# Moving the preparation of exponential tables to earlier batches of a projection stretch

## The chip, the core and the metric

The kernel runs on one core of one Trainium2 chip. A core has a tensor engine (PE, matrix products and transposes, with its weight loads shown as PEld), a vector engine (DVE), a scalar engine (ACT, activations and copies), GpSimd (POOL) and a queue engine (SP) that only issues transfers. Sixteen DMA engines move data between the chip's memory and the core. Each engine takes its own instructions in order; they wait for one another through semaphores. The metric is device time in microseconds (us), lower being better. All arrays are float32.

## The reference

The input x has 64 rows in the batch, 128 channels and 2048 steps in time. Two residual layers follow each other:

```python
# layer 0: each batch row picks one of 16 weight matrices of 128 x 128
x = x + einsum('bct,bcd->bdt', x, weights[condition])
# layer 1: a long convolution along time, one kernel K per channel, cut off at a length per row
dt  = exp(log_dt);  dtA = (-exp(log_A_real) + 1j * A_imag) * dt
Ct  = Cc * (exp(dtA) - 1) / A
K   = 2 * einsum('hn,hnl->hl', Ct, exp(dtA[:, :, None] * arange(2048))).real
y   = causal convolution of x with K, plus x * D
x   = x + y * (arange(2048) < length)
```

`exp(dtA * step)` is a damped turning number for each of 128 channels and 64 modes. The kernel does not convolve over all 2048 steps at once. It cuts time into chunks of 128 steps, uses a Toeplitz matrix inside a chunk, and carries 64 complex states from chunk to chunk. For both it needs tables of those turning numbers for 0 to 128 steps.

## The kernel before

**The two stretches.** Time is cut in two segments of 1024 steps. First, layer 0 is computed for segment 0 of all 64 rows ("batches" in the code, counted from 0): `batch0(b)`. After that the main loop goes over groups of channels; it computes layer 1 for both segments, and layer 0 for segment 1 in between. Layer 0 works with channels on the partitions and layer 1 with batch rows on them, so the result goes out to a scratch array `scr` in the chip's memory and comes back as `x` tiles. The first such load needs every row of segment 0.

**A batch of the first stretch.** `batch0(b)` does the following in order. Every second batch, SP fetches a pair of rows 9 pairs ahead (`xb`, 1 MB, ten buffers). POOL copies the weights of batch b + 3 (`weigh`; four buffers). PE makes two products of 128 x 512 into a PSUM tile (two of them alternate). An engine that is passed in as `copy` brings the tile back into `xb`, and the ACT queue stores 512 KB to `scr`. The default for `copy` is ACT.

**The preparation of the tables.** Between the batches, in an order that is written out by hand, the engines prepare the tables. `_Parameters` computes rates, frequencies and phases on DVE during batches 0 to 11. `exps(g)` writes the damping part of table g with four ACT exponentials; there are 16 tables `e`. `partial_angles(k)` for k = 0 to 5 forms partial turns on DVE in six steps, five of them over 128 x 1600 elements, in the tile `parts`. Then each table takes ten steps of its own, the dictionary `STEPS`: a PE transpose of a slice of `parts` (`turn_parts`, tile `pa`), its copy by ACT (`keep_parts`, tile `a`), a PE product that adds the partial turns (`add_parts`, tile `pt`), four small DVE steps (`angles`), two sines on ACT (`sines`), two products on DVE (`products`), eight small PE products with output weights (`lags`, tile `pk`), a copy by ACT, one DVE addition, and two POOL stores of the convolution kernel to `kpad`. The key of `STEPS` is the lag in batches behind the table's first step. A new table starts every second batch, beginning with batch `FIRST`.

**What sets the order.** Nothing is reordered by a scheduler. Each engine runs its instructions as the Python code emits them, and `manual_schedule` adds the semaphores. ACT needs a table load of its own whenever it changes between exponentials and sines.

**Lines of the change.** Lines 596 to 612 emit the parameters and batches 0 to 11; `exps(b - 6)` in batches 6 to 9 writes tables 0 to 3. Lines 743 to 777 are the loop over batches 12 to 63. In batches 12 to 17, the copy is DVE's, one step of `partial_angles` follows, and two tables of exponentials are written. POOL issues sixteen tiny loads of the gains `dcol` in batches 12 to 19, two a batch. The first table starts with batch 18; the last one, started with batch 48, ends its lags with batch 55 and its stores with batch 60.

Of the kernel before, what the change touches and what calls it, by code (L numbers as in the profile page):

```python
# [371 lines left out]
def cond_resid_ssm_kernel(  # L372
# [13 lines left out]
    nc = tc.nc  # L386
# [47 lines left out]
    def fetch(s, n):  # L434

        xbs[s, n] = big.tile([P, BT, SL], F32, tag="x", name=f"xb_{s}_{n}")
        src = x[n * BT : (n + 1) * BT, :, s * SL : (s + 1) * SL]
        nc.sync.dma_start(xbs[s, n], src.rearrange("b c t -> c b t"))

    def weigh(s, b, plus=None):  # L440

        w1s[s, b] = s0.tile([P, C], F32, tag="w1", name=f"w1_{s}_{b}")
        at = nc.values_load(
            ci[:, b : b + 1],
            engines=(mybir.EngineType.Pool,),
            min_val=0,
            max_val=S - 1,
            skip_runtime_bounds_check_because="it is clamped above",
        )
        w = wres[:, bass.ds(at, 1), :].rearrange("p s d -> p (s d)")  # L450
        if plus is None:
            nc.gpsimd.tensor_copy(w1s[s, b], w)  # L452
        else:
            nc.gpsimd.tensor_tensor(w1s[s, b], w, plus, ALU.add)

    def project(s, b, q, ps, n_banks=1, copy=nc.scalar.copy):

        n, r = divmod(b, BT)
        own = xbs[s, n][:, r, :]
        for k in range(n_banks):  # L460
            cols = slice((q + k) * BK, (q + k + 1) * BK)
            nc.tensor.matmul(ps[:, k], w1s[s, b], own[:, cols], start=True, stop=True)  # L462
        cols = slice(q * BK, (q + n_banks) * BK)
        copy(own[:, cols], ps.rearrange("p k t -> p (k t)"))  # L464
        if q + n_banks == QB:
            to = scr[s].rearrange("(f b) c t -> b c f t", f=2)[b]
            nc.scalar.dma_start(to, own.rearrange("c (f t) -> c f t", f=2))
            del w1s[s, b]
            if r == BT - 1:
                del xbs[s, n]  # L470

    def batch0(b, copy=nc.scalar.copy):
        if b % BT == 0 and b // BT + AHEAD < B // BT:
            fetch(0, b // BT + AHEAD)
        if b + WAHEAD < B:
            weigh(0, b + WAHEAD)
        project(0, b, 0, psp.tile([P, QB, BK], F32, tag="y", name=f"p0_0_{b}", bufs=2), QB, copy)

    V = nc.vector
    es = [tab.tile([P, TP, 2, NE], F32, tag=f"e{g}", name=f"e_{g}") for g in range(NT)]  # L480

    def par_of(row, g, i):
        return gtab[:, row, g * TP + i : g * TP + i + 1]

    def exps(g):

        for i in range(TP):
            nc.scalar.activation(es[g][:, i, 0, :], steps, AF.Exp, scale=par_of(DRE, g, i))
# [12 lines left out]
    with tc.tile_pool(name="setup", bufs=1) as setup:  # L501
# [47 lines left out]
        def run(chain, n=None):  # L549
            for _ in chain if n is None else zip(range(n), chain):  # L550
                pass
# [53 lines left out]
        par.lay("ppar_2", rows, 1, par.row(gtab, PHI))  # L605
        run(par.sizes())
        batch0(10)
        rows = par.spread("rows3", (par.amp, 1.0), (par.amp, -1.0), (par.lr, 1.0), (par.li, 1.0))
        batch0(11)
        par.lay("ppar_3", rows, 4, par.row(ptab, AMP), swapped=1)  # L610
        rows = par.spread("rows4", (par.wr, 1.0), (par.wi, 1.0))
        par.lay("ppar_4", rows, 2, par.weight)
# [9 lines left out]
    def partial_angles(k):  # L622

        own = parts[:, :, 0:NL]
        by_l = some_l.unsqueeze(1).to_broadcast([P, NP, NL])

        def of(row, n):
            return gtab[:, row, :].unsqueeze(2).to_broadcast([P, NP, n])

        if k == 0:  # L630
            V.tensor_tensor(own, of(FHI, NL), by_l, ALU.mult)
        elif k == 1:
            V.tensor_scalar(whole, own, MAGIC, MAGIC, ALU.add, ALU.subtract)
        elif k == 2:
            V.tensor_tensor(own, own, whole, ALU.subtract)
        elif k == 3:
            V.tensor_tensor(whole, of(FLO, NL), by_l, ALU.mult)
        elif k == 4:
            V.tensor_tensor(own, own, whole, ALU.add)
        else:  # L640
            V.tensor_tensor(parts[:, :, 0:8], parts[:, :, 0:8], of(PHI, 8), ALU.add)
            V.tensor_tensor(parts[:, :, 24:25], parts[:, :, 24:25], of(PHI, 1), ALU.add)
            V.tensor_scalar(last, parts[:, :, 24:25], MAGIC, MAGIC, ALU.add, ALU.subtract)
            V.tensor_tensor(last, parts[:, :, 24:25], last, ALU.subtract)
# [83 lines left out]
    def fetches(n):  # L728

        nonlocal begun  # L730
        while begun < min(n + BT * QB, len(pieces)):
            fetch(pieces[begun][0], pieces[begun][1] // BT)
            begun += BT * QB
# [7 lines left out]


    ps = {}
    FIRST = 18
    STEPS = {
        12: store_lags,
        10: gain_lags,
# [7 lines left out]
        0: turn_parts,  # L755
    }
    for now in range(12, B):
        batch0(now, V.tensor_copy if now < 18 else nc.scalar.copy)
        if now < 20:

            by_row = d_in.rearrange("(h j c d) -> c d j h", j=8, c=2, d=2)
            with nc.allow_non_contiguous_dma(reason="128 gains, four times"):
                for i, r in ((i, r) for i in range(TP) for r in range(4) if (i * 4 + r) // 2 == now - 12):
                    nc.gpsimd.dma_start(dcol[i * NR + r : (i + 1) * NR : 4, :], by_row[r % 2, r // 2])
        if now == 21:
            V.tensor_scalar(dcol, dcol, 1.0, None, ALU.add)
        if now < FIRST:
            partial_angles(now - 12)
        if now < 18:
            exps(2 * now - 20)  # L770
            exps(2 * now - 19)
        for lag, step in STEPS.items():
            g, odd = divmod(now - FIRST - lag, 2)
            if not odd and 0 <= g < NT:
                step(g)
        if now == 60:
            fetches(FILL)
# [232 lines left out]
```

## Time and profile before

| what | value |
|---|---|
| three runs, median (lowest to highest) | 1125.23 us (1122.19 to 1125.81) |
| the profiled execution, its own time | 1122.48 us |
| its span in the profile | 1120.7 us |
| PE busy, share of the span | 1076.6 us, 96% |
| DVE, ACT, POOL busy | 803.0, 680.7, 242.5 us |
| matmuls of layer 0 (`p`, L462) | 257.9 us, 512 records, 617 ns mean |
| exponentials of the tables (`e`, L488) | 64, 385 to 406 ns each, from 33.7 to 71.7 us |
| copies of `parts` slices (`a`, L653) | 16, 266 ns each, from 75.1 to 153.4 us |
| first load of `x` back from `scr` | issued at 186.19 us, landed 5.79 us later |

The span starts with the first instruction and ends with the last; the execution's own time is a little more. A line of the profile names the engine, the source line, the operation, and its output and input tiles. The chain of waits goes back from the last instruction to whatever released each step. A window row gives each engine's busy time in a stretch, the granted PE clock and what DMA moved. A record of a product of 512 columns is half of it: "p L462 x4" is one batch, that is two products.

### The profile page before, as it was taken

What the parts mean: (1) busy time and instruction counts of PE and PEld (TensorE: products, weight loads), DVE (VectorE), ACT (ScalarE), POOL (GpSimd) and SP (SyncE); (2) the same over time, 40 slices, a digit from 0 to 9 for tenths busy, and PEclk for the clock granted to TensorE, in tenths of its full rate; (3) what the DMA queues carried; (4) which work ended last, traced back from release to release, by engine and by line L of the source; (5) the groups of instructions that cost most, each with busy time, mean ns of one, the idle gap of its engine ahead of it and who ended that gap; (6) DMA issues with size and microseconds to landing.
All of it is one profiled execution on the core that took longest, in us unless ns stands there. A gap on an engine that the chain in (4) does not pass through costs nothing.

```text
span 1120.7 us, 23853 instructions
## 1 busy us (share of the span) xinstructions
PE 1076.6 (96%) x8634; PEld 786.6 (70%) x8634; DVE 803.0 (72%) x2671; ACT 680.7 (61%) x1123; POOL 242.5 (22%) x421
## 2 busy tenths in 40 slices
PE   5779998999999999999999999999999999999996
PEld 2224443677777777777777778888888888888885
DVE  7656550467657667667666758888888888888886
ACT  3577665766666566566566566665566566556652
POOL 3253332121221212122122211211211111121110
PEclk9899999999999999999999999999999999999999
DMA  9999999999999999999999887787787887788754
GB/s 346 415 398 386 409 410 379 357 281 285 344 280 294 298 293 298 302 299 281 293 299 284 260 264 212 225 228 226 229 228 210 237 230 223 216 240 228 210 166 118
DMA packets 117126, 313.25 MB, mean 280 GB/s; under 512 B 11858, under 2 KB 11986, under 8 KB 108818
## 3 DMA queue, kind: packets, MB, share of 16 engines
q1 hardware_dynamic: 70928, 218.65, 62.1%
q10 hardware_dynamic: 35106, 67.64, 16.1%
q0 software_dynamic: 10976, 25.45, 8.9%
q8 instruction: 68, 1.11, 0.4%
q14 instruction: 48, 0.39, 0.1%
HBM read 164.76 MB, written 146.93 MB: 278 GB/s over the span
## 4 chain that ended last, share of the span: by engine, by line
PE 91%; DMA 3%; DVE 2%; ACT 1%; issue 1%; ACTq 0%; SPq 0%; POOLq 0%; DVEq 0%
PE y L911 21%; PE y L899 20%; PE v L858 18%; PE p L462 17%; PE tr L833 10%; DMA xb<-in_x_dram 2%; PE pb L815 2%; PE pt L660 1%; DMA scr<-xb 1%; PE pk L690 1%; DVE s L873 1%; DMA x<-scr 1%; ACT xb L464 0%; DVE xb L464 0%; DVE x L920 0%
## 5 line engine op out<-in xcount | busy, mean ns | idle before, releaser
L873 DVE SCALAR_TENSOR_TENSOR s<-s,ptab 128x128 f32<-128x128 f32 x1792 | 520.2, 343 | 109.0 <-ACT s L863 92.7
L863 ACT ACTIVATE s<-v,ptab 64x512 f32<-64x512 f32 (+1 forms) x512 | 336.0, 656 | 50.4 <-PE v L858 33.9
L899 PEld LDWEIGHTS y<-tt,u 128*128 128x128 f32 x2048 | 263.5, 192 | 80.5 <-issue 67.0
L462 PE MATMUL p<-xb,w 128*128 128x512 f32 x512 | 257.9, 617 | 22.4 <-DMA xb<-in_x_dram 10.9
L899 PE MATMUL y<-tt,u 128*128 128x128 f32 x2048 | 269.9, 275 | 0.1
L911 PEld LDWEIGHTS y<-e,s 64*128 64x128 f32 x4096 | 233.9, 188 | 46.6 <-issue 24.2
L858 PE MATMUL v<-u,bt 128*128 128x512 f32 (+1 forms) x512 | 248.6, 567 | 0.0
L911 PE MATMUL y<-e,s 64*128 64x128 f32 x4096 | 246.7, 275 | 1.4 <-DVE s L873 1.4
L834 ACT COPY u<-tr 128x512 f32<-128x512 f32 x256 | 150.5, 588 | 156.6 <-PE tr L833 130.2
L882 DVE TENSOR_SCALAR s<-s 128x128 f32<-128x128 f32 x448 | 98.8, 221 | 137.6 <-ACT s L863 137.6
L464 ACT COPY xb<-p 128x512 f32<-128x512 f32 (+1 forms) x186 | 133.4, 718 | 83.9 <-PE p L462 80.7
L920 DVE COPY_PREDICATED x<-mask,y 128x1024 f32<-128x1024 uint8 x128 | 166.5, 1301 | 1.1 <-PE y L911 1.0
L833 PEld LDWEIGHTS tr<-ident,x 128*128 128x128 f32 x1024 | 121.6, 141 | 54.8 <-issue 49.3
L833 PE MATMUL tr<-ident,x 128*128 128x128 f32 x1024 | 156.3, 275 | 3.9 <-DMA x<-scr 3.9
L462 PEld LDWEIGHTS p<-xb,w 128*128 128x128 f32 x512 | 87.9, 197 | 89.3 <-issue 80.1
L452 POOL COPY w<-wres 128x128 f32 x125 | 58.6, 469 | 291.7 <-PE p L462 291.3
L801 POOL DMA_DIRECT2D tt<-kpad x64 | 50.5, 789 | 207.3 <-DVE s L873 168.0
L858 PEld LDWEIGHTS v<-u,bt 128*128 128x128 f32 x512 | 79.9, 192 | 13.9 <-issue 13.6
L846 POOL DMA_DIRECT2D s<-carry x64 | 44.9, 706 | 126.1 <-PE y L911 121.4
L816 ACT COPY bt<-pb 128x512 f32<-128x512 f32 x32 | 18.8, 586 | 87.5 <-PE pb L815 86.7
L890 POOL DMA_DIRECT2D carry<-s x64 | 43.6, 721 | 69.7 <-DVE s L873 63.6
L843 POOL MEMSET s<- 128x384 f32 x32 | 14.8, 462 | 149.4 <-DMA carry<-s 66.6
(199 smaller groups left out, 296.1 us busy)
## 6 DMA issues: line engine op xcount, KB each, us to landing
xb<-in_x_dram SPq DMA_DIRECT2D x64, 1024.0 KB, 10.1
scr<-xb ACTq DMA_DIRECT2D x128, 512.0 KB, 8.3
x<-scr SPq DMA_DIRECT2D x64, 1024.0 KB, 8.1
out_dram<-x SPq DMA_DIRECT2D x126, 512.0 KB, 4.8
tt<-kpad POOLq DMA_DIRECT2D x64, 256.0 KB, 5.9
btd<-bt SPq DMA_DIRECT2D x32, 256.0 KB, 7.2
bt<-btd SPq DMA_DIRECT2D x32, 256.0 KB, 4.9
carry<-s POOLq DMA_DIRECT2D x64, 64.0 KB, 7.1
```

Of the source, the lines that this page charges most:

```text
L452: nc.gpsimd.tensor_copy(w1s[s, b], w)
L462: nc.tensor.matmul(ps[:, k], w1s[s, b], own[:, cols], start=True, stop=True)
L464: copy(own[:, cols], ps.rearrange("p k t -> p (k t)"))
L833: nc.tensor.transpose(tr[:, k, :], xs[i][:, c, k * Q : (k + 1) * Q], ident)
L834: nc.scalar.copy(u, tr)
L858: nc.tensor.matmul(v[:, 0:nv], w, us[i, n].rearrange("p k r -> p (k r)")[:, 0:nv], start=True, stop=True)
L863: nc.scalar.activation(own[:, 0:nv], v[lanes, 0:nv], AF.Copy, scale=amp)
L873: nc.vector.scalar_tensor_tensor(new[:, d, 0:2], src, factor, own[:, d, 0:2], ALU.mult, ALU.add)
L882: nc.vector.tensor_scalar(old[:, :, 2], old[:, :, 0], -1.0, None, ALU.mult)
L899: nc.tensor.matmul(y[:, k, :], u[:, k, :], tts[i][:, n, :], start=(k == 0), stop=False, skip_group_check=True)
L911: nc.tensor.matmul(ys[i, d][:, c, k, :], st[half[c], d, part, k, :, :].rearrange("p f b -> p (f b)"), e[half[c], pair % TP, part, 0:Q], st ...
L920: nc.vector.copy_predicated(xs[i][:, d::2, :].rearrange("r c (k t) -> r c k t", k=KK), keep_k.unsqueeze(1).to_broadcast([P, 2, KK, Q]), ys ...
```

## The change

The six steps of `partial_angles` go from batches 12 to 17 to batches 12 to 14, two a batch. The tables begin with batch 15 in place of 18, and so end with batch 57 in place of 60. Tables 4 and 5 get their exponentials in batches 10 and 11; the others follow two a batch, one batch earlier than before, and end with batch 16. The copies of batches 13 and 14 go from DVE to ACT; DVE keeps those of 12 and of 15 to 17. What is computed is the same, and no step is added or taken away.

```diff
         batch0(10)
+        exps(4)
         rows = par.spread("rows3", (par.amp, 1.0), (par.amp, -1.0), (par.lr, 1.0), (par.li, 1.0))
         batch0(11)
+        exps(5)
...
     ps = {}
-    FIRST = 18
+    FIRST = 15
+    WHEN = {12: (0, 1), 13: (2, 3), 14: (4, 5)}
...
     for now in range(12, B):
-        batch0(now, V.tensor_copy if now < 18 else nc.scalar.copy)
+        batch0(now, V.tensor_copy if 14 < now < 18 or now == 12 else nc.scalar.copy)
...
-        if now < FIRST:
-            partial_angles(now - 12)
-        if now < 18:
-            exps(2 * now - 20)
-            exps(2 * now - 19)
+        for k in WHEN.get(now, ()):
+            partial_angles(k)
+        if now < 17:
+            exps(2 * now - 18)
+            exps(2 * now - 17)
```

## The prediction

> **What bounds the kernel now.** The page comes first. Its 40 slices of 28 us show what DMA moved: 346 to 415 GB/s in the first seven, the stretch that projects the first half of the sequence, and far less behind it, where the tensor engine (PE) is busy 9 tenths everywhere:
>
> ```profile
> GB/s 346 415 398 386 409 410 379 357 281 285 344 280 294 298 293 298 302 299 281 293 299 284 260 264 212 225 228 226 229 228 210 237 230 223 216 240 228 210 166 118
> ```
>
> The change touches only the first 166 us. What it does there reaches the end through one gate: the first load of x back from scratch waits for every store of the stretch. The chain of waits passes it at 186.19 us; after that PE work follows PE work, so a microsecond at the gate is a microsecond of the run.
>
> Next the windows by stage. Columns: length, then PE, PEld, DVE, ACT and POOL busy us (count), granted PE clock, DMA share, GB/s. The first rows are cut to the clock's own steps of 3.41 us, which show as changes of the granted clock:
>
> ```profile
> 45.54:48.95 3.41, 0.73 (x4) 0.54 (x4) 2.83 (x15) 1.34 (x2) 0.92 (x2) 1.00 1.03 414
> 48.95:52.36 3.41, 3.23 (x6) 1.70 (x7) 0.75 (x4) 0.00 (x0) 0.00 (x0) 0.50 1.04 409
> ...
> 66.02:69.43 3.41, 1.68 (x5) 0.56 (x4) 2.94 (x6) 2.70 (x10) 3.37 (x6) 1.00 1.05 406
> 69.43:72.84 3.41, 1.16 (x3) 0.19 (x1) 0.00 (x0) 3.24 (x9) 0.29 (x1) 1.00 1.03 405
> 72.84:76.26 3.42, 3.21 (x4) 1.51 (x5) 0.17 (x1) 1.39 (x3) 0.00 (x0) 0.50 1.04 400
> 76.26:100.00 23.74, 22.73 (x88) 9.37 (x90) 13.37 (x27) 16.27 (x24) 3.72 (x9) 1.00 1.02 371
> 100.00:165.00 65.00, 65.00 (x344) 28.19 (x344) 39.23 (x84) 44.96 (x74) 25.93 (x52) 1.00 1.04 409
> 165.00:186.00 21.00, 20.50 (x62) 8.65 (x62) 0.59 (x2) 12.47 (x17) 6.30 (x18) 1.00 1.03 400
> ```
>
> The reader is to see two limits side by side. From 100 to 165 us PE never stops and DMA moves 409 GB/s, near the 415 of the page's best slice. From 76 to 100 us DMA drops to 371: (409 - 371) x 23.7 us = 0.90 MB, or 2.2 us at 409. The chain gives the PE pace in between:
>
> ```profile
> 90.21 1.91 PE p L462 x4
> 92.12 0.86 PE pt L660 x2
> 92.98 0.11 PE pa L649
> 93.09 1.72 PE p L462 x4
> 94.81 0.58 PE pk L690 x16
> ...
> 165.90 15.66 PE p L462 x36
> ```
>
> Two batches and one table take 5.18 us on PE. Their transfers, 2 x 1.05 MB, take 5.12 us at 409. So PE leads by 1%, and which batches carry tables matters. From 165.9 us the tables are over, PE runs a batch in 1.74 us, and stores alone set the pace.
>
> **The jam before the tables.** The timelines of ACT and DVE show why PE is idle and half-clocked around 70 us:
>
> ```profile
> 54.54 1.28 ACT L488 ACT_TABLE_LOAD   x1 [7.22 <-DVE xb L464]
> ...
> 59.07 3.90 ACT L488 ACTIVATE e<-steps,gtab 128x129 f32<-128x129 f32 x13
> ...
> 71.96 0.99 ACT L464 COPY xb<-p 128x1024 f32<-128x1024 f32 x1
> ```
>
> ```profile
> 54.03 1.82 DVE L631 TENSOR_TENSOR parts<-gtab,some_l 128x1600 f32<-128x1600 f32 x1
> 55.76 1.22 DVE L464 COPY xb<-p 128x1024 f32<-128x1024 f32 x1
> 56.90 0.98 DVE L633 TENSOR_SCALAR whole<-parts 128x1600 f32<-128x1600 f32 x1
> ```
>
> Columns: start, us, engine, line, operation, output and input; the square bracket gives idle time and what ended it. ACT idles 7.22 us up to 54.5, then runs 48 exponentials (13 in 3.90 us, 0.30 each) until 71.96, and only then copies batch 18 (all batches are counted from 0, as in the code). PE waits for that copy, because two PSUM buffers alternate.
>
> **Part 1: the exponentials of tables 4 and 5 in batches 10 and 11.** Nothing is added: eight ACTIVATEs and one table load (1.28 us, the row above) move into the idle 7.22 us. Batch 11's copy, at 46.31 now, comes 1.28 + 1.2 = 2.5 us later; its store was issued only at 50.82, so the cover is 1.9 us wide after the copy and nothing is lost. Gain on ACT: 1.28 + 2.4 = 3.7 us before 72.
>
> **Part 2: two partial operations a batch in 12 to 14, and copies 13 and 14 on ACT.** DVE drops two copies (1.22 each) and runs the six steps in a row after batch 12's copy, from 54.03: 1.85 + 1.0 + 3 x 1.85 + 1.5 = 9.9 us (the durations of the timeline, with the short wait between dependent steps). It ends at 63.9 instead of 69.0. ACT takes two copies of 1.01 us, each with 0.44 us before its store. On ACT, in order: table pair 6, 7 until 56.9; copy 13 to 58.0 (now done at 57.0 by DVE); pair 8, 9 to 60.9; copy 14 to 61.9 (now 59.0); pair 10, 11 to 64.8. Behind copy 14 stands PE's batch 16, behind copy 13 batch 15; so two PSUM releases come 1.0 and 2.9 us later than now. POOL's eight gain loads and its weight copies keep their order, and so do SP's fetches; a fetch needs two landed stores, and batch 14's store is the late one, so the fetch behind it moves by about 1 us, which 8.4 us of normal time to landing covers.
>
> **Part 3: tables from batch 15.** Batch 15's copy stays on DVE and now stands behind all six steps: 63.9 to 65.1 (now 60.7 to 61.9). PE's first transpose waits for the steps (63.4), and batch 16 stands behind it. Exponentials 12, 13 stand behind the store of 15 (65.1) on ACT: 65.5 to 67.9. Batch 16 on PE is done by 67.1, if its window is at half clock; its copy ends at 68.3, its store goes, and exponentials 14, 15 end at 71.1. The first `a` copy stands behind them: 71.4 instead of 75.4. The product that opens table 0 runs at 71.4 instead of 76.4, 5 us earlier, where three batches would be 7.8.
>
> Here a rule of the Trainium skill is weighed ("TensorE: Matmul & The Clock Gate", "What's actually happening"): the clock falls to half only after a whole idle window of about 3.4 us. The rows differ: a window with 1.16 of 3.41 us busy (34%) was followed by 0.50, one with 1.68 (49%) by 1.00. In the changed kernel PE has about 0.6 us in 59.2 to 62.6 (batch 15's tail). By the rule batch 16 runs at full clock and is done at 65.4; by the rows it takes 3.4 us and is done at 67.1. I take the rows. Exponentials 14 and 15 stand between, so only 0.8 us of the 1.7 reach the first `a`: by the rule the lag below is 0.8 us and the run 1125.9, by the rows 1.6 us and 1126.7.
>
> From there PE carries the path: batch 18 at 72.4 to 74.1, its copy from 74.1 (now 71.96), then 1.73 a batch, 0.86 + 0.11 a table and, from batch 22, 0.58; one further wait of 1.3 us where the third `a` stands behind the sine load (1.28) and sines (1.3) on ACT. Adding on, batch 27's store is issued at about 97.5, against 95.95 now: **1.6 us late**, but with one and a half tables more done (3 products, 3 lags: 2.3 us of PE).
>
> **The sum.** Before, batch 52 is stored at 160.4 with one and a half tables to go; in the changed kernel it comes 1.6 us later, with none to go. Batches 53 to 55 then run no faster than their transfers, 3.15 MB or 7.7 us at 409, against 3 x 2.59 = 7.8 us at the pace with tables now. So the tables' head start is worth 0.1 us, the lag stays, and the gate moves by +1.5 us, from 186.2 to 187.7. Bounds: the late copies could be hidden by transfers already queued (8.4 us from issue to landing at the steady pace, while the last stores of the stretch land in 5 us at 400 GB/s): 0. The other end is one more window at half clock, 1.7 us, since 69.43 to 72.84 would hold only 1.4 us of PE work (41%, between the two rows): +3.3.
>
> The profiled execution took 1122.48 us, 1.8 more than its span of 1120.7; it would become 1124.0. The runs have a median of 1125.23, so **1126.7**, 0.13% slower. A difference under 0.3% (3.4 us) I call none; the three runs spread by that much.
>
> **Rivals.** First, *the dip closes.* The 371 GB/s fall exactly behind the jam of 60 to 72 us. If stores and fetches flow evenly there, 2.2 us come back, and 65 us at 415 in place of 409 give 1.0: 3.2, with what is left of the half-clock window at most 4. Time: 1122.0, and 1121.2 at its best. For it: ACT's 7.2 idle us are used, PE idles 6.9 of the 20.5 us in the six windows from 55.78 to 76.26. Against: copies 13 to 16 are later, not earlier, and DMA cannot pass 415. Chance 0.27.
>
> Second, *ACT is the jam again, and slower.* The place is the first `a`, behind exponentials 14 and 15 and, through two stores, behind DVE copies. If it comes later than about 73 us, PE has a second window under 40% busy and half clock takes another 1.7 us; with 1 us of waiting the lag is 1.6 + 1.7 + 1 = 4.3: 1129.5. For it: the 34% row. Against: nothing on ACT is added but two copies, and 3.7 us are freed. Chance 0.29.
>
> Third, *it doesn't matter, DMA sets the gate.* If queued transfers absorb the lag, the time is 1125.2. This lies within the forecast's own range, 1124.5 to 1128.6; together 0.44.
>
> **The numbers.** The likeliest case gives 1126.7. The range takes in the middle of both rivals, 1121.7 to 1130.5. Faster by over 0.3% needs under 1121.9: the better part of rival 1, 0.20. Slower by over 0.3% needs over 1128.6: rival 2 and the last tail of the forecast, 0.33. The rest is 0.47.
>
> **What would show it.** ACT's idle time before 54.5 gone and a table load near 46; six DVE steps in one run ending near 64; the first `a` near 71; a half-clock step near 63; batch 27's store near 97.5; the tables' last product near batch 52; the gate near 187.7. A gate before 184, or the 76 to 100 us row at 400 GB/s, would prove rival 1; a gate after 190, rival 2.

## The result and the profile after

The changed kernel takes **1130.97 us** (median of 17 runs, 1124.86 to 1136.2) against 1124.94 us for the kernel before (17 runs, 1120.82 to 1130.11): ratio **1.0058, 95% interval [1.0038, 1.0078]**, so slower by 4 to 9 us. The prediction said 1126.7, at most 1130.5. The profiled execution took 1132.8 us, with a span of 1131.0.

| profiled execution, us | before | after | difference |
|---|---|---|---|
| store of batch 27 issued | 95.95 | 99.20 | +3.25 |
| from there to the store of batch 52 | 64.43 | 68.16 | +3.73 |
| from there to the first load of x | 25.81 | 25.91 | +0.10 |
| first load of x, the gate | 186.19 | 193.27 | +7.08 |
| its landing, and the first transpose | 5.93 | 8.86 | +2.93 |
| from there to the end of the span | 928.6 | 928.9 | +0.3 |

Of the 10.3 us between the two spans, 7.08 lie ahead of the gate. The stretch from the load to the first transpose varied from 5.4 to 8.9 us over the kernels profiled here, whatever was changed, and is left out below.

The windows by stage of the changed kernel, with the columns of before, show two places:

```profile
59.35:62.76 3.41, 0.97 (x3) 0.14 (x1) 3.38 (x2) 2.97 (x9) 2.50 (x5) 1.00 1.03 407
62.76:66.18 3.42, 2.45 (x4) 1.28 (x5) 2.50 (x6) 2.53 (x10) 0.00 (x0) 0.50 0.99 303
66.18:69.59 3.41, 3.41 (x5) 1.35 (x4) 1.22 (x1) 2.35 (x9) 1.38 (x3) 0.50 1.01 396
...
76.41:100.00 23.59, 22.59 (x99) 9.77 (x99) 14.02 (x29) 16.95 (x27) 5.33 (x12) 1.00 0.98 358
100.00:165.00 65.00, 63.02 (x337) 26.60 (x336) 36.85 (x79) 42.21 (x69) 24.31 (x51) 1.00 1.03 384
```

First, PE is at half clock for two steps, 62.76 to 69.59, where one was forecast. Second, and not forecast at all, PE is not full any more from 100 to 165 us: 63.02 of 65.00, and DMA moves 384 GB/s instead of 409. A pace that was to be left alone has changed.

The preparation itself went as worked out. PE's timeline has the first transpose at 63.73 (63.4 forecast), batch 16 up to 67.6 at half clock (its row also holds batch 17), and the first product of table 0 at 71.98 (71.4):

```profile
63.73 0.47 PE L651 MATMUL pa<-ident,parts 128*128 128x128 f32 x1 [3.41 <-DVE parts L644]
63.99 6.38 PE L462 MATMUL p<-xb,w 128*128 128x512 f32 x8
71.98 1.13 PE L662 MATMUL pt<-pick,a 128*128 128x512 f32 x2 [1.60 <-ACT a L655]
```

ACT's timeline has the table load at 46.77, the first `a` at 71.68 (71.4 forecast), the copy of batch 18 at 74.97 (74.1), and then something new, a wait in the steady stretch:

```profile
46.77 1.28 ACT L488 ACT_TABLE_LOAD   x1 [0.43 <-ACT xb L464]
...
71.68 0.24 ACT L655 COPY a<-pa 128x128 f32<-128x128 f32 x1
74.97 1.01 ACT L464 COPY xb<-p 128x1024 f32<-128x1024 f32 x1 [3.04 <-PE p L462]
...
103.33 1.01 ACT L464 COPY xb<-p 128x1024 f32<-128x1024 f32 x1 [0.71 <-PE p L462]
104.95 0.37 ACTq L467 DMA_DIRECT2D scr<-xb  x1
105.41 0.27 ACT L698 COPY krow<-pk 128x128 f32<-128x128 f32 x1 [1.06 <-DMA xb<-in_x_dram]
```

The store of batch 29 stands at the head of ACT's queue. Its copy was done at 104.34; it is issued at 104.95. What it waits for is a **fetch**, which no line of the code asks for. Everything behind it on ACT waits too. The groups of ACT from 100 to 165 us add it up. Before:

```profile
L464 ACT COPY xb<-p 128x1024 f32<-128x1024 f32 x26 | 26.2, 1007 | 8.9 <-PE p L462 8.9
...
L696 ACT COPY krow<-pk 128x128 f32<-128x128 f32 x12 | 3.2, 266 | 6.0 <-ACT xb L464 6.0
```

After:

```profile
L464 ACT COPY xb<-p 128x1024 f32<-128x1024 f32 x24 | 24.2, 1007 | 6.6 <-PE p L462 6.5
...
L698 ACT COPY krow<-pk 128x128 f32<-128x128 f32 x11 | 2.9, 266 | 9.8 <-DMA xb<-in_x_dram 7.3 <-ACT xb L464 2.5
```

7.3 us of waiting for fetches have appeared and two batches fewer are done in the same 65 us. The chain of waits of the changed kernel passes through one of these waits:

```profile
127.65 1.93 PE p L462 x4
129.60 0.71 ACT xb L464
130.31 8.13 DMA xb<-in_x_dram
138.48 0.04 issue
138.52 0.37 ACTq L467
```

A fetch of 8.13 us lands at 138.44, and 0.08 later the store of batch 41 goes out.

**Where the wait comes from.** Transfers that SP and ACT issue signal their landing on eight semaphores in rotation, as the instruction records show. A transfer waits until the one eight places earlier has landed, since it uses the same semaphore. So the order in which fetches and stores stand decides which store waits for which fetch. In the built programs (s = store of a batch, f = fetch of a pair):

```
before: ... s24 f21 s25 s26 f22 s27 s28 f23 ...   store 2k-12 waits for fetch k  (s26 for f19, s28 for f20)
after:  ... f21 s24 s25 f22 s26 s27 f23 s28 ...   store 2k-13 waits for fetch k  (s25 for f19, s27 for f20)
```

Fetch k itself waits for store 2k-19, because the ten buffers `xb` have to come free. The two waits make a ring: seven batches long before, six after. The trace of after shows one turn after another: store of batch 23 lands at 97.63, fetch 21 goes out at 97.71 and lands at 104.87, store 29 goes out at 104.95; store 41 lands at 145.12, fetch 30 goes out at 145.20; store 47 lands at 160.76, fetch 33 goes out at 160.84 and lands at 169.98, store 53 goes out at 170.05. From the store of batch 23 (88.84) to that of batch 53 (170.05) there are five turns of 16.24 us, 2.71 us a batch. At PE's pace, 2.588 (two batches and a table in 5.18), six batches last 15.5 us, less than a turn; seven last 18.1, more. The long ring is slack, the short one binds.

What made the order change is the parity of the batch in which tables begin: 18 before, 15 after; in all eight kernels of the table below that have no added transfers, an even start has the long ring from batch 30 on and an odd one the short ring. (The long order of before holds from store 26 on; up to store 23 it has the short one too.) In the code a fetch is emitted ahead of its pair's stores in both kernels, so the order of before is not that of the code. How the places are given is not shown here.

### The profile page after: what moved, and what is told of

The parts are those of the page before. It is cut to its first block, busy times and chain, and to the rows that moved or that the text cites. A ratio compares the mean times of both kernels' runs of the same rounds, so it can differ in the third digit from the quotient of the medians.

```text
span 1131.0 us, 23855 instructions
## 1 busy us (share of the span) xinstructions
PE 1077.8 (95%) x8634; PEld 786.5 (70%) x8634; DVE 800.8 (71%) x2669; ACT 682.6 (60%) x1125; POOL 239.5 (21%) x421
## 4 chain that ended last, share of the span: by engine, by line
PE 90%; DMA 3%; ACT 2%; DVE 2%; issue 1%; ACTq 0%; POOL 0%; POOLq 0%; DVEq 0%; SPq 0%
PE y L914 21%; PE y L902 20%; PE v L861 18%; PE p L462 17%; PE tr L836 10%; PE pb L818 2%; DMA scr<-xb 1%; PE pt L662 1%; ACT xb L464 1%; DMA x<-scr 1%; DMA xb<-in_x_dram 1%; PE pk L692 1%; ACT e L488 1%; DVE s L876 1%; DMA wres<-in_L_cond_weights_dram 1%
## 5 line engine op out<-in xcount | busy, mean ns | idle before, releaser
L452 POOL COPY w<-wres 128x128 f32 x125 | 54.6, 437 | 304.3 <-PE p L462 303.2
```

## The experiments

Two causes were held: a **lag** of some 3 us at batch 27 from the early start, and the **short ring** behind it. Rivals: the moved preparation itself costs time; or an odd start is slow by its place on PE, with no part played by the semaphores. Each kernel was run against the kernel before, 6 (e5, e7) to 22 times. The columns from "batch 27" on are of one profiled execution each; "pace" is us a batch from the store of batch 32 to that of batch 44, where all kernels have tables. "Ring" is what the built program has in that stretch: its length in batches, or "none" where no store waits for a fetch. A gate in one execution says little below 1.5 us: e4's is 1.6 and e15's 1.4 us later than before, with no loss in the runs.

| kernel | ring | batch 27 | pace | gate | ratio to before, 95% |
|---|---|---|---|---|---|
| before | 7 | 95.95 | 2.588 | 186.19 | 1 |
| after | 6 | 99.20 | 2.793 | 193.27 | 1.0058 [1.0038, 1.0078] |
| e1 after, ring broken | none | 98.95 | 2.589 | 190.01 | 1.0036 [1.0024, 1.0048] |
| e2 after, start 16 | 7 | 95.34 | 2.588 | 185.02 | 1.0012 [0.9996, 1.0028] |
| e3 before, start 19 | 6 | 95.20 | 2.643 | 189.03 | 1.003 [1.0016, 1.0045] |
| e4 before, exponentials moved | 7 | 98.18 | 2.588 | 187.77 | 1.0003 [0.9988, 1.0017] |
| e5 e3, small transfers | none | 99.11 | 2.609 | 194.85 | 1.0079 [1.0054, 1.0104] |
| e6 e1, extra products | none | 100.34 | 2.588 | 192.54 | 1.0056 [1.0036, 1.0077] |
| e7 e1, table 0 later | none | 106.53 | 2.588 | 197.61 | 1.0079 [1.0054, 1.0105] |
| e8 after, start 14 | 7 | 102.06 | 2.588 | 191.79 | 1.0053 [1.0032, 1.0073] |
| e9 e3, broken from batch 28 | none | 96.48 | 2.598 | 196.94 | 1.007 [1.0045, 1.0095] |
| e10 after, broken from 16 | none | 98.49 | 2.588 | 195.12 | 1.006 [1.0038, 1.0082] |
| e11 after, start 17 | 6 | 99.58 | 2.663 | 192.71 | 1.0066 [1.0044, 1.0088] |
| e12 after, start 18 | 7 | 96.92 | 2.588 | 186.22 | 1.0013 [0.9995, 1.0031] |
| e13 e9, ended at batch 46 | none | 96.49 | 2.598 | 190.25 | 1.0047 [1.003, 1.0064] |
| e14 e10, ended at batch 46 | none | 97.78 | 2.588 | 191.11 | 1.0026 [1.0013, 1.0039] |
| e15 before, small transfers | none | 96.02 | 2.588 | 187.63 | 1.0002 [0.9984, 1.002] |

### The two causes apart: e1, e2, e3

e1 puts a 64-byte transfer of SP behind each pair of batches while fetches last; its rows go nowhere. It takes a place in the rotation, and with it no store of the steady stretch stands eight places behind a fetch.

```diff
+        t = s0.tile([1, 16], F32, tag="tick", name=f"tick_{b}", bufs=4)
+        nc.sync.dma_start(t, x[0:1, 0, 0:16])
```

> The changed kernel with one more transfer of 64 bytes on SP in every second batch from batch 12, nothing else. Eight semaphores go round over the transfers of SP and ACT, so with four transfers a pair in place of three a store waits for the store two pairs ahead of it and no longer for a fetch. Ring theory (in the changed kernel store b waits for a fetch that waits for store b-6, so six batches per 16 us, 2.7 us a batch): the steady pace goes back to 2.59 us and 3.5 to 4 of the 6.5 us lost come back, ratio to before 1.002 to 1.003, 1127 to 1128.5 us. Theory of the prediction (a lag made before batch 27 by the late copies and by PE's clock): nothing comes back, ratio 1.0058, or a little more for the added transfers.

The pace is 2.589 again, and the groups of ACT from 100 to 165 us of e1 show 26 copies and no wait for a fetch:

```profile
L469 ACT COPY xb<-p 128x1024 f32<-128x1024 f32 x26 | 26.2, 1007 | 11.4 <-PE p L467 10.9 <-ACT xb L469 0.4
...
L705 ACT COPY krow<-pk 128x128 f32<-128x128 f32 x12 | 3.2, 266 | 5.9 <-ACT xb L469 5.9
```

Batch 27 stays late (98.95). Cured of the ring in this stretch, the change still costs 0.36%. (At its end the last small transfer leaves store 48 behind fetch 31, until 155.99; by batch 52 that is made up, 3.0 us late as at batch 27.)

e2 moves only the start, to an even batch (`FIRST = 16`), and e3 moves only the start of the kernel before, to an odd one (`FIRST = 19`, with the partial angles left in batches 12 to 17).

> The changed kernel with the tables begun at batch 16 in place of 15; everything else as changed. With an even start the order of fetches and stores is that of before: store b waits for the fetch behind store b-7. Ring theory: the steady pace is 2.59 us a batch, 1126 to 1128 us, ratio 1.001 to 1.003. Theory of the prediction: the preparation and its late copies are the same, one batch later matters by under 1 us, ratio 1.005 to 1.006.

> The kernel before with the tables begun at batch 19 in place of 18, nothing else of the change. An odd start gives the short ring of six batches. Ring theory: the pace of the steady stretch is 2.7 us a batch, 3 to 4 us slower, ratio 1.003 to 1.0035. Theory of the prediction: the preparation is untouched and the tables have one batch more to be ready, so no change, ratio 0.999 to 1.001.

e2 has neither a lag nor the short ring, and no slowdown that could be measured. e3 has no lag (95.20), but the short ring, and is 0.3% slower. Its ACT groups show the same wait, in a kernel that has nothing of the change in it but the parity:

```profile
L696 ACT COPY krow<-pk 128x128 f32<-128x128 f32 x12 | 3.2, 266 | 9.9 <-DMA xb<-in_x_dram 6.5 <-ACT xb L464 3.4
```

So ring alone (e3) 0.30%, lag alone (e1) 0.36%, both (after) 0.58%, neither (e2) 0.12% with an interval that holds zero. The intervals of e1 and after overlap, so the ring's share in the time rests on e3; e1 shows it in the pace.

e2 also answers the forecast's first rival. From 76 to 100 us its windows move the 411 GB/s that were to bring back 2.2 us and more:

```profile
76.00:100.00 24.00, 23.08 (x115) 9.89 (x114) 15.51 (x33) 17.33 (x28) 5.57 (x11) 1.00 1.04 411
100.00:165.00 65.00, 65.00 (x329) 27.98 (x329) 35.55 (x77) 43.76 (x72) 26.01 (x54) 1.00 1.04 405
```

Batch 27 is 0.6 us earlier, no more. PE is 96% busy in that stretch with the dip (before) and without it (e2), so what DMA catches up there is hardly time.

### The ring by itself: e5, e9, e13, e10, e14, e15

e5 puts the small transfers of e1 into e3.

> The kernel before with the tables begun at batch 19 and the 64-byte transfer in every second batch. Ring theory: the odd start was slow (ratio 1.003) only through the short ring, so the added transfer takes it back to 1.000 to 1.001, with a steady pace of 2.58 us a batch. If an odd start is slow for another reason (table steps falling on the batches without a fetch): still 1.003, or more for the added transfers.

A miss, and a useful one: the pace is nearly right (2.609), but the small transfers made shorter rings at both ends. In the built program store 20 waits for fetch 17, and where the small transfers end, store 48 for fetch 31. That fetch went out at 150.17 and landed at 158.01; store 48 went out at 158.09. e9 and e10 were to avoid it with other first batches, the transfers running on to batch 62:

```diff
+        if b % BT == 0 and 28 <= b < 64:
+            tick(b)
```

> The kernel before with tables from batch 19, as in e3 (odd start), and with one 64-byte SP transfer behind each pair of batches from batch 28 to the end of the stretch, so that from batch 30 no store waits for a fetch. Here the small transfers make no shorter ring at either end, unlike e5. Ring theory: the pace of batches 30 to 52 returns from 2.71 to about 2.58 us a batch, the gate comes at 186 to 187 instead of 189.0, ratio to before 1.000 to 1.0015. Rival (the odd start is slower because PE's table products fall on the batches without a fetch, whatever the semaphores do): pace 2.70, gate 189, ratio 1.003 as in e3.

> The changed kernel with the same small SP transfers from batch 16 to the end of the stretch; no store from batch 18 on waits for a fetch. Two-part theory (early lag of about 3 us at batch 27, plus a short ring worth about 3 us afterwards): only the lag is left; batch 27 stored near 98.5 to 99, pace 2.58, gate near 189 to 190, ratio 1.002 to 1.0035. If the lag too comes from stores waiting for fetches: batch 27 before 97, ratio below 1.001.

Between the ends both paces came as the ring theory said, 2.598 and 2.588; the ratios did not. With no fetches left to pace them the last small transfers ran in a burst (eight in e9 within 4.2 us) and held up the stores. ACT's timeline of e9 shows both prices, at the first transfer and at the burst:

```profile
107.82 0.27 ACT L660 COPY a<-pa 128x128 f32<-128x128 f32 x1 [3.45 <-DMA xb<-in_x_dram]
...
156.15 0.27 ACT L660 COPY a<-pa 128x128 f32<-128x128 f32 x1 [5.95 <-DMA scr<-xb]
```

e13 and e14 repeat them with `b < 48`, and e15 puts small transfers (batches 28 to 44) into the kernel before.

> As e9 (the kernel before with tables from batch 19, small SP transfers from batch 28), but they end with batch 46, where the fetches end; the only store behind batch 23 that waits for a fetch is that of batch 30. Ring theory: batch 36 at about 119.5 to 121, pace of batches 36 to 52 2.55 to 2.6 instead of 2.75, gate 186.5 to 188, ratio 1.000 to 1.002. Rival (an odd start is slow by its place on PE): gate 189, ratio 1.003.

> As e10 (the changed kernel with small SP transfers from batch 16), but they end with batch 46; no store behind batch 17 waits for a fetch. Two-part theory: batch 27 at 98.5 to 99, pace 2.58 to batch 52, gate 189 to 190, ratio 1.0025 to 1.0035, as e1. Rival (the ring isn't it): pace 2.7, gate 192 to 193, ratio 1.005.

> The kernel before (even start, long ring) with the small SP transfers in batches 28 to 44. Ring theory: a ring of seven batches doesn't hold back anything, so breaking it gains nothing, and 64 bytes a pair of batches cost nothing: pace 2.57 to 2.59, gate 186 to 187, ratio 0.999 to 1.001. If the small transfers bring something of their own (a kinder order of transfers): ratio below 0.998, and e1 can't be read as the ring's share.

e14 came as expected in ratio, 1.0026, the second kernel beside e1 in which only the lag is left. (Its gate, 191.1, is later than expected; 3.1 us of waiting at the last small transfers are in it.) e15 shows that small transfers bring nothing: 1.0002, and the same pace. Its insertion cost 2 us (batch 32 at 110.70 against 108.73). e13 missed its ratio. ACT's timeline has why, two stalls at the ends again, the first of them in the place of e9's:

```profile
107.91 0.27 ACT L660 COPY a<-pa 128x128 f32<-128x128 f32 x1 [3.52 <-DMA xb<-in_x_dram]
...
151.05 0.27 ACT L660 COPY a<-pa 128x128 f32<-128x128 f32 x1 [2.47 <-DMA tick<-in_x_dram]
```

Whole times of e5, e9, e10 and e13 thus price the tool as well as the ring. What holds over all kernels is the column of paces: the nine kernels with the small transfers have 2.588 to 2.609 there, among them three with the odd start of e3; the five with a seven-batch ring 2.588; the three with the short ring 2.643, 2.663 and 2.793. An odd start with the ring broken runs at PE's pace, so the rival "place on PE" falls. That the short ring seems to cost after more (2.793) than e3 (2.643) lies in the stretch chosen. From batch 27 to batch 52 the three take 67.8 (e3), 68.2 (after) and 67.8 us (e11), that is 2.71 to 2.73 us a batch, which is the turn of 16.24 us for six batches; before and e1 take 64.4.

### The lag: e8, e6, e7

e8 begins tables with batch 14, even, hence with the long ring.

> The changed kernel with the tables begun at batch 14 in place of 15; no added transfer. An even start, so the long ring and a steady pace of 2.58 us. But batch 15's product now stands behind the first transpose, which waits for the last partial operation at 63.7 us, so store 15 at 67 or later and a lag of 3 to 6 us at batch 27: ratio 1.003 to 1.005. If the ring were all of the loss: 1.001.

Pace 2.588, and the lag doubles: batch 27 at 102.06, 6.1 us late. ACT's timeline shows the wait, exponentials behind the store of a batch whose product waits for the partial angles:

```profile
69.31 2.46 ACT L488 ACTIVATE e<-steps,gtab 128x129 f32<-128x129 f32 x8 [4.41 <-DVE xb L464]
```

So a batch more of early start costs 3 us more, without any short ring, and a batch less (e2) takes the lag away. PE's timelines show what goes with it. The first transpose waits for the partial angles, and a batch's product stands behind it: PE idles 3.41 us ahead of it in after, 7.13 us in e8, and not at all in e2, where batch 16's product goes first. In e8:

```profile
63.72 0.47 PE L651 MATMUL pa<-ident,parts 128*128 128x128 f32 x1 [7.13 <-DVE parts L644]
```

In e2:

```profile
63.40 0.27 PE L651 MATMUL pa<-ident,parts 128*128 128x128 f32 x1
```

e6 adds four unread products in batch 15 to e1, to keep the clock up.

```diff
+                extra = psp.tile([P, TP, Q], F32, tag="v", name=f"warm_{k}", bufs=2)
+                for _ in range(2):
+                    nc.tensor.matmul(
```

> The changed kernel with the added transfer, and with four matmuls of 128x512 that nobody reads put on PE in batch 15, between its product and the first transpose of parts, where PE waits from about 60.3 to 63.7 us. They keep PE busy, not early. If the lag of 3 us at batch 27 comes from the two half-clock windows at 62 to 69 us: these go, store 18 comes near 74 in place of 75.8, ratio 1.0015 to 1.0025 in place of 1.0036. If it comes from the waits behind the transpose and the late copies alone: 1.0036 as without them.

The steps at half clock at 62 us went, and one came at 71.7 to 75.1 in their place; the first `a` is at 71.1 (71.4 in e1), since the exponentials hold it, and batch 18 is later, 77.2. Full clock for batch 16 alone does not help. The traces of e10 and e14 happened to have one step at half clock near 65 instead of two, and lags of 2.5 and 1.8 us. That fits the second step being worth about 1 us, but other waits differ too.

e7 lets table 0 alone run one batch later, in e1:

```diff
-            if not odd and 0 <= g < NT:
+            if not odd and 0 < g < NT:
                 step(g)
+            if now == FIRST + lag + 1:
+                step(0)
```

> The changed kernel with the added transfer, and table 0 alone one batch later: its transpose stands behind batch 16's product and its first product behind batch 18's; tables 1 to 15, the partial operations, exponentials and copies stay as changed. If the lag comes from batches 16 and 18 standing behind table 0 on PE: store 18 at 71 to 72 us, ratio 1.000 to 1.0015. If it comes from the late copies 13 and 14 on ACT: store 18 at 75 and ratio 1.0036 as without.

A miss in time: the order of transfers changed (store 18 waits for fetch 16, store 20 for 17, 22 for 18), and from batch 18 to batch 22 the stores take 17.4 us instead of 10.3 in e1. But ACT's timelines show the lag ahead of that. The copy of batch 18 starts here at

```profile
72.44 1.02 ACT L469 COPY xb<-p 128x1024 f32<-128x1024 f32 x1
```

and in e1 at

```profile
74.72 1.01 ACT L469 COPY xb<-p 128x1024 f32<-128x1024 f32 x1 [3.04 <-PE p L467]
```

against 71.96 before. So of e1's 2.8 us at batch 18, 2.3 are gone once table 0 no longer stands ahead of that batch on PE; its store then waits for fetch 16, up to 74.39. The lag is thus, in the main, batches that stand on PE behind the first steps of table 0, and these wait for the partial angles and, at the first `a`, for exponentials on ACT. The shares of these waits, of the late copy of batch 14 and of the clock are not settled.

### Parts of the preparation: e4, e12, e11

e4 moves only the exponentials in the kernel before; e12 does everything that the change does but starts tables with batch 18; e11 with 17.

> The kernel before with the exponentials of tables 4 and 5 in batches 10 and 11 and the others one batch earlier; partial operations, copies and the tables' start at 18 as before. Ring theory: the order of fetches and stores in the steady stretch stays that of before, no change or a gain of up to 2 us from ACT's idle time that is used, ratio 0.998 to 1.0005. Theory of the prediction for this part: nothing lost, up to 3.7 us of ACT time freed, ratio 0.998 to 1.000. If moving the exponentials is itself the harm: 1.003 or more.

> The changed kernel with its tables from batch 18, as before: all that the change does to the preparation, but neither an earlier nor an odd start. Two-part theory: no lag, long ring: batch 27 stored at 94 to 96, pace 2.55 to 2.58, gate 185 to 186.5, ratio 0.998 to 1.001. If the moved preparation itself costs time (copies 13 and 14 on ACT, exponentials behind them): batch 27 later than 97, ratio 1.0015 or more.

> The changed kernel with its tables from batch 17 instead of 15: odd start again, so the short ring, but batches 16 and 18 don't stand behind table 0 on PE. Two-part theory: no lag (batch 27 stored at 95 to 96), pace 2.71, gate 188 to 189.5, ratio 1.002 to 1.0035. If what matters is only how early the tables start: between e2 (batch 16) and before, 1.000 to 1.001.

In time e4 and e12 are no different from before within their intervals: the moved preparation costs nothing that could be measured, and brings nothing. In e4 ACT's timeline shows what takes back the time that it freed:

```profile
76.69 0.27 ACT L655 COPY a<-pa 128x128 f32<-128x128 f32 x1 [4.54 <-DMA xb<-in_x_dram]
```

Batch 18 is stored 2.5 us earlier (70.45), and the store of batch 19, whose copy is done at 72.14, then stands behind a fetch until 76.00: stores that are ready sooner meet the same rotation. e11 has the short ring, as expected, but not the early batch 27: ACT waited 3.93 us for fetch 17 at the store of batch 21, so that a wait of the same kind had struck before batch 27 already. Its ratio, 1.0066, is above what was expected of it.

No kernel tried was faster than the one before by more than can be measured.

## Why the prediction was wrong

- **Preparation.** Right to within half a microsecond: table load at 46.8, DVE's steps to 64.2, batch 16 at half clock, first `a` at 71.7, tables over with batch 52. (One sum was off without effect: with a copy of 1.0 us, the cover over batch 11's store is 50.82 - 46.31 - 2.5 - 1.0 = 1.0 us, not 1.9. It held: that store went out at 51.07.)
- **The clock.** The rows were the better guide: 0.97 of 3.41 us busy was followed by 0.50, as the 34% row said. But one step at half clock was charged, and there were two. The second was the upper bound's term, 1.7 us, put at 69 to 73; it fell at 66.2 to 69.6.
- **The lag**, predicted 1.6 us at batch 27, was 3.25 in the profile of after, near the upper bound of 3.3, and 1.8 to 3.0 in the kernels that differ only in broken rings. The term was too small; its direction and place were right. Of the 1.7 us missing at batch 27, 0.9 are there by the copy of batch 18 (74.97 against 74.1), behind the second step at half clock; the rest is not traced.
- **The step that failed** is in the sum: batch 52 "comes 1.6 us later", the lag of batch 27 carried on with nothing added, so the pace behind batch 27 was taken as that of before. It rested on SP's fetches, which were to keep their order, with a delay that 8.4 us to landing covers. The order of fetches among themselves did stay; their place among the stores did not, and with it went the batch of slack between fetch and store. That cost 3.73 us from batch 27 to batch 52, more than everything forecast, and was in no bound.
- **The head start** of the tables was put at a gain of 0.1 us; behind batch 52 after takes 0.10 us longer. Nothing either way, as the forecast said in substance.
- **Rivals.** A gate after 190 was to prove rival 2. It came (193.3) without rival 2's condition, a first `a` after 73; half of the loss has another cause. That sign did not tell apart what it was to tell apart. Rival 1 is answered by e2; the 415 GB/s that "DMA cannot pass" were only the best slice of 28 us, since from 40 to 45 us before moved 419. Rival 3, that DMA takes up the lag, fails in e1 and e8: lags of 3.0 and 6.1 us at batch 27 are 3.8 and 5.6 at the gate.

## What to carry to other kernels

Where several queues share a few completion semaphores in rotation, write down for each transfer what stands that many places ahead of it: such a wait appears in no line of the code, and moving *any* transfer by one place, or starting a two-batch pattern on an odd batch, can close it to a ring with a buffer wait. A ring is judged by its batches times the pace, against one store landing plus one fetch landing, before the pace is taken as unchanged. A transfer put in to break a ring has two ends, where it makes new ones.

## What was not expected of the hardware

- A step at half clock was followed by another although PE was busy for 2.45 of its 3.42 us (72%, the idle part at its start); with 2.92 of 3.41 us (86%, 49.11 to 52.52 in the same profile) full clock came back. The 992 steps of 3.41 us between the first fall of the clock and 230 us in the 17 profiles divide cleanly by PE's busy share. Those at full clock were followed by half clock up to 39% (1.33 us, e14, 61.37 to 64.78), by full clock from 47%. Those at half clock were followed by half clock up to 80% (2.74 us, e15, 35.19 to 38.60), by full clock from 81%. No full-clock step lies between 39 and 47%.
- Landing takes long in the full stream: stores 4.9 to 9.1 us, fetches 7.2 to 9.3 us from 88 to 165 us in after (those on seven of the eight semaphores), with 384 GB/s moved. That is why a ring of two landings could reach six batches of work.
- The runs of after spread over 11.3 us (1124.86 to 1136.2), those of before over 9.3 us in the same comparison. The spread is larger than the effect; only the number of runs tells them apart.
